# Two layers of attention with two-level fast products: outer additions queued behind VectorE's urgent reads, statistics read in attention, first factors in one transfer each

## The chip, the cores and the metric

The kernel runs on one core of one Trainium2 chip. The metric is the device time of one execution in microseconds (us): 3364.67 for the kernel before, the median of 3 runs (3364.36 to 3367.72). The profiled execution has a span of 3367.4 us.

A core has TensorE (matrix products into the accumulators of PSUM), VectorE, ScalarE and GpSimd, which work at the same time, each through its own list of instructions in the order in which the program gives them, and transfers (DMA), which are issued from a list of their own, SyncE's. In the profile they are PE (and PEld for the loading of weights), DVE, ACT, POOL and SP.

## The reference

Eight samples of 512 channels by 32 x 32 positions go through two attention layers. A layer is, cut to what matters:

```python
xn  = group_norm(x)                        # 8 groups of 64 channels, over all positions
q, k, v = wq @ xn + bq, wk @ xn + bk, wv @ xn + bv
attn = softmax(q_head . k_head * scale)    # 8 heads of 64 channels, 1024 x 1024 each
out  = attn . v_head
x    = x + wp @ out + bp
```

Everything is fp32. A sample in a layer is a *job*; the 16 jobs run in the order (sample 0, layer 0), (1, 0), (0, 1), (1, 1), (2, 0) and so on, so that the job two places after one in layer 0 is the same sample in layer 1.

## The kernel before

The four projections of a job are computed with Strassen-like products: a product of matrices of 2 x 2 blocks with 7 block products and additions of the factors before and of the results after. V and the output projection do it once. K and Q do it twice: seven outer products, each a *chain* of seven inner products. The sums of the weights (*factors*) are made once per layer and kept in HBM.

One job's stages: attention of job n; the V products of job n+1; the output projection of job n; the K and Q products of job n+1 (14 chains). One instruction list of VectorE serves all of this. `later` and `advance` are a plan in Python, without effect on the chip: they decide at which place in the program's order an operation is put.

The chains of K and Q. `step` does one inner product and the reading of an accumulator bank that belongs to it; products 7 and 3 are read by VectorE, the others by ScalarE:

```python
        def step(o):
            product(o, {1: z, 5: w, 6: z, 2: y, 7: z, 3: u, 4: z}[o], o in (1, 5))
            if o == 1:
                nc.scalar.copy(y, z)
            elif o == 5:
                put5(w)
            elif o == 6:
                nc.scalar.copy(u, z)
            elif o == 2:
                put(0, 0, y)
            elif o == 7:
                put(1, 1, z)        # VectorE
            elif o == 3:
                put(0, 1, u)        # VectorE
            else:
                put(1, 0, z)        # ScalarE
```

Each chain's result is a tile of pool `e`; the *outer additions* put these results together into k or q as soon as a chain has ended:

```python
        def end(c):
            ...
            if o == 2:
                nc.vector.tensor_add(quarter(0, 0), p(1), p(2))
            elif o == 6:
                nc.vector.tensor_add(p(6), p(6), p(1))
            elif o == 5:
                nc.vector.tensor_add(quarter(0, 1), p(6), p(5))
            elif o == 7:
                nc.vector.tensor_add(p(7), p(7), p(6))
                nc.vector.tensor_add(quarter(1, 1), p(7), p(5))
            ...
        def thunk(c, j):
            def go():
                if j == 0:
                    live[c] = begin(c)
                live[c](ORDER[j])        # ORDER = (1, 5, 6, 2, 7, 3, 4)
                if j == 6:
                    end(c)
                advance(0.43)
            return go

        at = sorted((7 * c + 2 * j, c, j) for c in range(len(chains)) for j in range(7))
```

By the last line the chains overlap: after the end of chain c (place 7c+12) come product 2 of chain c+1 (7c+13), product 1 of c+2, product 7 of c+1 (7c+15), product 5 of c+2, product 3 of c+1 (7c+17).

Results of chains and the exponentials of attention share one pool of buffers:

```python
    epool = ctx.enter_context(tc.tile_pool(name="epool", bufs=LEAD + 2))   # LEAD = 2
    ...
            e = epool.tile([P, 2, HALF], F32, tag="e", name=f"e_{n}_{i}")
            nc.scalar.activation(e, sc, AF.Exp, scale=SCALE)
```

The inner factors of K and Q are made when a layer is first met (jobs 0 and 2): the pieces are fetched from the stored outer factors, four small additions on VectorE make the rest (`prepare`), and the whole is stored:

```python
    def fetch():
        if not plan:
            return
        ...
        if which in (V, O):
            nc.sync.dma_start(wide(w), src)
        elif (which, layer, o) in deep:
            nc.sync.dma_start(w, deep[which, layer, o])
        else:
            for at, i, j in ((A11, 0, 0), (A12, 0, 1), (A22, 1, 1), (S3, 1, 0)):
                nc.sync.dma_start(w[:, at], src[:, j, i * P : (i + 1) * P])
            raw.add(key)
```

In job 0 the outer factors are made on the way, too. Raw K, raw Q and the finished k are tiles with the same tag "k" of a pool with one buffer: each needs the one before to be done with. The same holds for raw V and q (tag "q"):

```python
    store_factors(v0, 0, V)
    first_blocks(k0, 0, K, 0.1)
    deep_sums(0, 7.0, 14.0)

    def second_blocks():
        q0 = acts.tile([P, NW, 2, CH], F32, tag="k", name="raw_q0")
        load_blocks(q0, 0, Q)
        first_blocks(q0, 0, Q, 6.0)
    ...
    later(7.5, first_plan)      # fetches K's seven pieces
    later(9.0, second_blocks)
```

The statistics of the next job's normalisation (four times two readings of 128 x 512 and one small operation) are put into attention for a job in layer 0, and among the chains before it for a job in layer 1:

```python
            reads, steps = norm_steps(n + 2)
            if jobs[n + 2][1] == 1:
                for i, step in enumerate(reads):
                    later(9.0 + 6.0 * i, step)
                reads = []
        ...
                chores = dict(zip((4, 8, 12, 16), reads))    # in attention
```

Of the kernel before, what the change touches and what calls it, by code (L numbers as in the profile page):

```python
# [18 lines left out]
P = 128  # L19
# [14 lines left out]
LEAD = 2  # L34
RP = 32
NQ = P // RP
CH = C // 2
A11, A12, A22, S1, S2, S3, S4 = range(7)
NW = 7
K, V, Q, O = range(4)  # L40
FACTOR = {1: A11, 2: A12, 3: S4, 4: A22, 5: S1, 6: S2, 7: S3}
# [28 lines left out]
def fast_path(  # L70
# [10 lines left out]
    nc = tc.nc  # L81
    xpool = ctx.enter_context(tc.tile_pool(name="xpool", bufs=2))
    acts = ctx.enter_context(tc.tile_pool(name="acts", bufs=1))
    epool = ctx.enter_context(tc.tile_pool(name="epool", bufs=LEAD + 2))
    apool = ctx.enter_context(tc.tile_pool(name="apool", bufs=2))
    small = ctx.enter_context(tc.tile_pool(name="small", bufs=2))
    dram = ctx.enter_context(tc.tile_pool(name="dram", bufs=2, space=DRAM))
# [19 lines left out]
    def advance(us):  # L107
        clock[0] += us
        due = [t for t in todo if t[0] <= clock[0]]
        for t in due:  # L110
            todo.remove(t)
            t[1]()
# [18 lines left out]
    def raw_block(layer, which, i, j):  # L131

        if which == O:
            w, at = wp[layer], 0
        else:
            w, at = wqkv[layer], {Q: 0, K: C, V: 2 * C}[which]
        cols = slice(at + i * CH, at + (i + 1) * CH)
        return w[j * CH : (j + 1) * CH, cols].rearrange("(cc p) o -> p cc o", p=P)
# [1 line left out]
    factors, deep = {}, {}  # L140

    def load_blocks(w, layer, which):
        for at, i, j in ((A11, 0, 0), (A12, 0, 1), (A22, 1, 1), (S3, 1, 0)):
            nc.sync.dma_start(w[:, at], raw_block(layer, which, i, j))

    def factor(w, part):

# [16 lines left out]
    def fetch():  # L164


        if not plan:
            return
        key = plan.popleft()
        n, which, o = key  # L170
        layer = jobs[n][1]
        w = ring.tile([P, NW, P], F32, tag="w", name=f"w_{which}_{n}_{o}")
        held[key] = w
        src = factors[which, layer][:, FACTOR[o]]
        if which in (V, O):
            nc.sync.dma_start(wide(w), src)
        elif (which, layer, o) in deep:
            nc.sync.dma_start(w, deep[which, layer, o])
        else:
            for at, i, j in ((A11, 0, 0), (A12, 0, 1), (A22, 1, 1), (S3, 1, 0)):  # L180
                nc.sync.dma_start(w[:, at], src[:, j, i * P : (i + 1) * P])
            raw.add(key)

    def prepare(key):
# [257 lines left out]
    def deep_phases(n):  # L442


        layer = jobs[n][1]
        dst = {}
        chains = [(K, o) for o in OUTER] + [(Q, o) for o in OUTER]
        tiles = {}

        def begin(c):  # L450
            which, o = chains[c]
            if o == OUTER[0]:
                name = "k" if which == K else "q"
                dst[which] = acts.tile([P, NC, S], F32, tag=name, name=f"{name}_{n}")
                (kt if which == K else qt)[0] = dst[which]
            if c + 2 < len(chains):
                prepare((n,) + chains[c + 2])
            e = epool.tile([P, 2, HALF], F32, tag="e", name=f"p_{n}_{c}")
            tiles[which, o] = e
            s5 = small.tile([P, QT], F32, tag="s5", name=f"s5_{n}_{c}", bufs=3)  # L460
            half = c % 2
            z, y, u, w = (
                bank(half, b, f"{b}d_{n}_{c}")[:, :QT] for b in ("vyuz", "zyuv")[(c // 2) % 2]
            )
            r = right(xn[0], tx[0], o)
            if o in (4, 5, 6):
                sums = deep_t[0][:, :, {5: 0, 6: 1, 4: 2}[o], :]
            else:
                at = {1: 0, 7: 1, 2: 2, 3: 3}[o]
                sums = deep_x[0][:, :, at, :]  # L470
            moving = {
                1: r[:, 0, :QT], 2: r[:, 1, :QT], 3: r[:, 1, QT:],
                5: sums[:, 0, :], 6: sums[:, 1, :], 7: sums[:, 2, :], 4: sums[:, 3, :],
            }
            lhs = held[n, which, o]

            def bias(oo):
                if o in (1, 6, 7):
                    return None
                if o == 3:  # L480
                    return bias_step[:, layer, int(which == Q), oo : oo + 1]
                oc = oo if o == 2 else 2 + oo
                return env.vec(layer, BK if which == K else BQ, oc)

            def product(i, ps, start):
                nc.tensor.matmul(  # L486
                    ps, lhs[:, FACTOR[i], :], moving[i], start=start, stop=True,
                    skip_group_check=True,
                )

            def put(oo, ph, ps):
                to_ = e[:, oo, ph * QT : (ph + 1) * QT]
                b = bias(oo)
                if ph == 0:
                    if b is None:
                        nc.scalar.copy(to_, ps)
                    else:
                        nc.scalar.activation(to_, ps, AF.Identity, bias=b)
                elif b is None:
                    nc.vector.tensor_add(to_, ps, s5)  # L500
                else:
                    nc.vector.scalar_tensor_tensor(to_, ps, b, s5, ALU.add, ALU.add)  # L502

            return chain(product, lambda ps: nc.scalar.copy(s5, ps), put, z, y, u, w)

        def end(c):
            which, o = chains[c]
            used((n, which, o))
            d = dst[which]

            def quarter(oh, sh):
                return d[:, 2 * oh : 2 * oh + 2, sh * HALF : (sh + 1) * HALF]

            def p(k):
                return tiles[which, k]

            if o == 2:
                nc.vector.tensor_add(quarter(0, 0), p(1), p(2))
            elif o == 6:
                nc.vector.tensor_add(p(6), p(6), p(1))  # L520
            elif o == 5:
                nc.vector.tensor_add(quarter(0, 1), p(6), p(5))
            elif o == 7:
                nc.vector.tensor_add(p(7), p(7), p(6))  # L524
                nc.vector.tensor_add(quarter(1, 1), p(7), p(5))
            elif o == 3:
                nc.vector.tensor_add(quarter(0, 1), quarter(0, 1), p(3))
            elif o == 4:
                nc.vector.tensor_add(quarter(1, 0), p(7), p(4))

        live = {}

        def thunk(c, j):
            def go():
                if j == 0:
                    live[c] = begin(c)
                live[c](ORDER[j])
                if j == 6:
                    end(c)
                advance(0.43)  # L540

            return go

        at = sorted((7 * c + 2 * j, c, j) for c in range(len(chains)) for j in range(7))
        return [thunk(c, j) for _, c, j in at]
# [181 lines left out]
    def first_blocks(w, layer, which, delay):  # L727

        for part in range(4):
            later(delay + 1.7 * part, lambda part=part: factor(w, part))  # L730
        later(delay + 6.0, lambda: store_factors(w, layer, which))

    def make_out_bias(w, layer):

        pb = two_banks("sc", f"pb_{layer}")
        for oc in range(NC):
            i, o0 = oc // 2, (oc % 2) * P
            for cc in range(NC):
                at = {(0, 0): A11, (0, 1): A12, (1, 0): S3, (1, 1): A22}[i, cc // 2]
                nc.tensor.matmul(  # L740
                    pb[:, 0, oc : oc + 1], w[:, at, cc % 2, o0 : o0 + P],
                    env.vec(layer, BV, cc), start=(cc == 0), stop=(cc == NC - 1),
                )
        a0 = layer * NVEC + BP
        nc.vector.tensor_add(out_bias[:, layer, :], pb[:, 0, :NC], env.vec_sb[:, a0 : a0 + NC])
# [51 lines left out]
    for step in (  # L797
# [1 line left out]
        lambda: factor(v0, 3), t[3],  # L799
    ):  # L800
        step()
    store_factors(v0, 0, V)
    first_blocks(k0, 0, K, 0.1)
    deep_sums(0, 7.0, 14.0)

    def second_blocks():
        q0 = acts.tile([P, NW, 2, CH], F32, tag="k", name="raw_q0")
        load_blocks(q0, 0, Q)
        first_blocks(q0, 0, Q, 6.0)

    def first_plan():
        plan.extend((0, K, o) for o in OUTER)
# [2 lines left out]

    def second_plan():
        plan.extend((0, Q, o) for o in OUTER)
        fetch()

    later(7.5, first_plan)  # L820
    later(9.0, second_blocks)
    for thunk in first[4:-1]:
        thunk()
    advance(0.0)
    rest = first[-1:]
    for n in range(-1, len(jobs)):
# [48 lines left out]
        reads = steps = []  # L875
        if n + 2 < len(jobs):
            reads, steps = norm_steps(n + 2)
            if jobs[n + 2][1] == 1:
                for i, step in enumerate(reads):
                    later(9.0 + 6.0 * i, step)  # L880
                reads = []
        for i, thunk in enumerate(both[1:-3]):
            if n < 0 and i == 14:
                second_plan()
            thunk()
        att_n = n + 1
# [252 lines left out]
```

## Time and profile before

| | |
|---|---|
| time, median of 3 runs | 3364.67 us |
| span of the profiled execution, mean granted TensorE clock | 3367.4 us, 0.995 |
| TensorE busy | 3286.2 us, 98% of the span |
| VectorE busy | 2602.4 us, 77% |
| ScalarE busy | 1727.5 us, 51% |
| moved by DMA | 262.83 MB, 78 GB/s over the span |
| chain of work that ended last | TensorE 90%, VectorE 6%, ScalarE 2%, DMA 1% |
| scores and values of attention in that chain | 26% and 25% |
| issues of pieces of K's and Q's factors (fetch) | 112 of 64 KB |

Busy time of an engine is the union of its instructions. In a group of instructions the idle time stands before them, with what ended it; a line of the timeline has its start, its length, engine, line of the program, tiles (out<-in), shapes, a count where neighbours are merged, and in brackets the engine's idle time before it and what it waited for. DMA issues stand on SyncE's queue (SPq); what they move lands later.

### The profile page before, as it was taken

The page shows a single profiled execution, that of the slowest core. Times are in us where ns is not written, and L with a number is a line of the kernel's source. Part 1 is how long each engine was busy: PE and PEld are TensorE (multiplying, and loading weights), DVE is VectorE, ACT ScalarE, POOL GpSimd, SP SyncE. Part 2 cuts the span into 40 slices and gives each one's busy share as a digit, 9 for nine tenths or more (in the row PEclk, how much of TensorE's full clock was granted, in tenths as well). Part 3 has the DMA queues.
Part 4 walks back from the last instruction along what each step waited for, and adds up shares of the span by engine and source line. Part 5 has one row for each costly group of instructions (what it writes and reads, how often), then busy time and mean ns, then how long its engine had stood idle before and what let it go on. Part 6 is the DMA issues. An engine that isn't in the chain of part 4 may idle for free.

```text
span 3367.4 us, 56688 instructions
## 1 busy us (share of the span) xinstructions
PE 3286.2 (98%) x22420; PEld 1742.5 (52%) x22420; DVE 2602.4 (77%) x3630; ACT 1727.5 (51%) x2557; POOL 17.5 (1%) x30
## 2 busy tenths in 40 slices
PE   7999999999999999999999999999999999999999
PEld 5446364463655636456374553735546365463643
DVE  6796977959688686786968869687795977968676
ACT  2554635646365463655636456363663635546363
POOL 0000000000000000000000000000000000000000
PEclk8999999999999999999999999999999999999999
DMA  6224132140411303114050220303215031130401
GB/s 237 91 84 130 62 105 86 57 160 18 129 60 41 101 22 100 38 51 138 22 161 28 66 75 22 115 24 96 93 34 161 18 89 50 40 102 18 125 29 44
DMA packets 154450, 262.83 MB, mean 78 GB/s; under 512 B 45888, under 2 KB 68416, under 8 KB 153152
## 3 DMA queue, kind: packets, MB, share of 16 engines
q1 hardware_dynamic: 154176, 259.12, 24.8%
q8 instruction: 178, 2.92, 0.4%
q14 instruction: 96, 0.79, 0.1%
HBM read 212.10 MB, written 44.83 MB: 76 GB/s over the span
## 4 chain that ended last, share of the span: by engine, by line
PE 90%; DVE 6%; ACT 2%; DMA 1%; issue 1%; SPq 0%; POOL 0%; DVEq 0%; ACTq 0%; POOLq 0%
PE sc L593 26%; PE po L618 25%; PE vd L486 6%; PE z L384 6%; PE z L419 6%; PE zd L486 6%; PE yd L486 2%; PE ud L486 2%; ACT e L598 2%; PE v L384 2%; PE y L384 2%; PE u L384 2%; PE y L419 2%; PE u L419 2%; PE v L419 2%; DVE p L524 1%
## 5 line engine op out<-in xcount | busy, mean ns | idle before, releaser
L598 ACT ACTIVATE e<-sc 128x1024 f32<-128x1024 f32 x1024 | 1045.7, 1023 | 640.9 <-PE sc L593 515.4
L593 PE MATMUL sc<-q,k 64*64 64x512 f32 x8192 | 1071.6, 593 | 16.0 <-ACT e L598 16.0
L618 PE MATMUL po<-e,v 64*64 64x512 f32 x8192 | 1060.2, 590 | 0.0
L604 DVE TENSOR_TENSOR acc<-acc,e 128x1024 f32<-128x1024 f32 x768 | 937.2, 1220 | 83.0 <-ACT e L598 32.6
L618 PEld LDWEIGHTS po<-e,v 64*64 64x64 f32 x8192 | 313.4, 134 | 568.4 <-issue 557.4
L593 PEld LDWEIGHTS sc<-q,k 64*64 64x64 f32 x8192 | 304.3, 133 | 563.1 <-issue 517.0
L486 PE MATMUL vd<-deep,w 128*128 128x256 f32 x960 | 278.0, 387 | 47.1 <-DVE p L502 30.6
L602 DVE TENSOR_TENSOR acc<-e,e 128x1024 f32<-128x1024 f32 x128 | 156.5, 1223 | 115.6 <-ACT e L598 114.4
L486 PE MATMUL zd<-deep,w 128*128 128x256 f32 x832 | 235.5, 383 | 6.9 <-DVE p L500 3.5
L486 PEld LDWEIGHTS vd<-deep,w 128*128 128x128 f32 x960 | 178.5, 191 | 99.3 <-DVE p L502 43.5
L486 PEld LDWEIGHTS zd<-deep,w 128*128 128x128 f32 x832 | 156.2, 190 | 43.2 <-DVE p L502 8.5
L630 DVE TRANSPOSE_TENSOR_REDUCE r<-acc 128x32 f32<-128x1024 f32 x128 | 158.5, 1238 | 0.6
L335 ACT COPY yd<-vd 128x256 f32<-128x256 f32 x128 | 45.7, 357 | 185.5 <-PE vd L486 178.2
L426 DVE TENSOR_TENSOR s5o<-v,x 128x512 f32<-128x512 f32 x60 | 38.6, 684 | 100.4 <-PE v L419 100.4
L419 PE MATMUL z<-to,w 128*128 128x512 f32 x240 | 110.4, 593 | 0.0
L384 PE MATMUL z<-w,xn 128*128 128x256 f32 x480 | 110.1, 383 | 0.0
L384 PE MATMUL z<-w,t 128*128 128x256 f32 x480 | 108.5, 379 | 0.0
L419 PE MATMUL z<-q,w 128*128 128x512 f32 x240 | 107.9, 593 | 0.0
L660 DVE TENSOR_TENSOR q<-q,rb 128x512 f32<-128x512 f32 x128 | 86.6, 677 | 27.5 <-DMA rb<-rd 27.5
L384 PEld LDWEIGHTS z<-w,xn 128*128 128x128 f32 x480 | 90.1, 190 | 23.7 <-issue 12.2
L384 PEld LDWEIGHTS z<-w,t 128*128 128x128 f32 x480 | 91.4, 190 | 12.2
L339 ACT COPY u<-z 128x512 f32<-128x512 f32 x62 | 35.3, 570 | 121.5 <-PE z L419 84.8
(176 smaller groups left out, 3434.7 us busy)
## 6 DMA issues: line engine op xcount, KB each, us to landing
w<-deep SPq DMA_DIRECT2D x196, 448.0 KB, 3.4
w<-keep SPq DMA_DIRECT2D x210, 256.0 KB, 2.7
rb<-rd SPq DMA_DIRECT2D x256, 128.0 KB, 2.9
x<-x_dram SPq DMA_DIRECT2D x32, 512.0 KB, 5.8
out_dram<-x SPq DMA_DIRECT2D x64, 256.0 KB, 3.6
deep<-w SPq DMA_DIRECT2D x28, 448.0 KB, 2.7
keep<-raw SPq DMA_DIRECT2D x5, 1792.0 KB, 5.9
lr<-r SPq DMA_DIRECT2D x512, 4.0 KB, 1.7
```

What stands on the lines that cost most here:

```text
L335: nc.scalar.copy(y, z)
L384: nc.tensor.matmul(ps[:, ti * CH : (ti + 1) * CH], r[:, cc, t0 : t0 + P], w[:, cc, :], start=(start and ti == 0 and cc == 0), stop=(cc == ...
L419: nc.tensor.matmul(ps, w[:, cc, i * P : (i + 1) * P], r[:, cc, :], start=(start and cc == 0), stop=(cc == 1), skip_group_check=True,)
L426: nc.vector.tensor_add(s5[:, oh, :], ps, at(oh, 1))
L486: nc.tensor.matmul(ps, lhs[:, FACTOR[i], :], moving[i], start=start, stop=True, skip_group_check=True,)
L593: nc.tensor.matmul(sc[h * HD : (h + 1) * HD, j, :], k[r, hp, k0 : k0 + HD], q[r, hp, sh * HALF : (sh + 1) * HALF], start=True, stop=True,)
L598: nc.scalar.activation(e, sc, AF.Exp, scale=SCALE)
L602: nc.vector.tensor_add(acc[g], es[i - 1], e)
L604: nc.vector.tensor_add(acc[g], acc[g], e)
L618: nc.tensor.matmul(po[g][j * HD : (j + 1) * HD, h, :], v[r, kc, d0 : d0 + HD], e[r, j, :], start=(kc == 0), stop=(kc == NT - 1),)
L630: nc.vector.tensor_reduce(r, a.rearrange("p j (b e) -> p (j b) e", e=RP), AX.X, ALU.add, apply_transpose=True,)
L660: nc.vector.tensor_mul(q[:, hp, cols], q[:, hp, cols], rb)
```

## The change

It leaves the computation as it is and touches the order and the transfers:

1. Outer additions are not given to VectorE at a chain's end. They go into a queue, and one is taken from it after each read of product 7 or 3 of the chains that follow, so that a read for which TensorE waits does not stand behind an addition for which nobody does. The rest is done at the end of the last chain. As results live longer, pool `e` gets a fifth buffer.
2. The statistics are read in attention for all jobs.
3. The blocks of a stored factor lie in the order in which a piece is used, so that a piece comes with one transfer, not four. In job 0 the order is another: K's outer factors are made at once, V's are stored much later, Q's blocks are loaded before K's pieces are fetched, and Q's pieces are fetched later and as many as the ring holds.

```diff
-A11, A12, A22, S1, S2, S3, S4 = range(7)
+A11, S3, A12, A22, S1, S2, S4 = range(7)
...
-    epool = ctx.enter_context(tc.tile_pool(name="epool", bufs=LEAD + 2))
+    epool = ctx.enter_context(tc.tile_pool(name="epool", bufs=LEAD + 3))
...
     def load_blocks(w, layer, which):
-        for at, i, j in ((A11, 0, 0), (A12, 0, 1), (A22, 1, 1), (S3, 1, 0)):
-            nc.sync.dma_start(w[:, at], raw_block(layer, which, i, j))
+        for i in range(2):
+            for j in range(2):
+                nc.sync.dma_start(w[:, 2 * j + i], raw_block(layer, which, i, j))
...
-        if not plan:
+        if not plan or len(held) == RING:
             return
...
         else:
-            for at, i, j in ((A11, 0, 0), (A12, 0, 1), (A22, 1, 1), (S3, 1, 0)):
-                nc.sync.dma_start(w[:, at], src[:, j, i * P : (i + 1) * P])
+            nc.sync.dma_start(wide(w), src)
             raw.add(key)
...
+            def add(to_, a, b):
+                outer.append(lambda: nc.vector.tensor_add(to_, a, b))
+
             if o == 2:
-                nc.vector.tensor_add(quarter(0, 0), p(1), p(2))
+                add(quarter(0, 0), p(1), p(2))
   ... (the other additions likewise)
         live = {}
+        outer = deque()
         def thunk(c, j):
             def go():
                 if j == 0:
                     live[c] = begin(c)
                 live[c](ORDER[j])
+                if ORDER[j] in (7, 3) and outer:
+                    outer.popleft()()
                 if j == 6:
                     end(c)
+                    if c + 1 == len(chains):
+                        while outer:
+                            outer.popleft()()
                 advance(0.43)
...
-        later(delay + 6.0, lambda: store_factors(w, layer, which))
+        later(delay + 5.3, lambda: store_factors(w, layer, which))
...
-    store_factors(v0, 0, V)
-    first_blocks(k0, 0, K, 0.1)
-    deep_sums(0, 7.0, 14.0)
+    for part in range(4):
+        factor(k0, part)
+    store_factors(k0, 0, K)
+    deep_sums(0, 0.5, 7.5)
...
-        first_blocks(q0, 0, Q, 6.0)
+        first_blocks(q0, 0, Q, 8.0)
...
     def second_plan():
         plan.extend((0, Q, o) for o in OUTER)
-        fetch()
-
-    later(7.5, first_plan)
+        while len(held) < RING and plan:
+            fetch()
+
+    later(12.0, first_plan)
     later(9.0, second_blocks)
+    later(35.0, lambda: store_factors(v0, 0, V))
...
-            if jobs[n + 2][1] == 1:
-                for i, step in enumerate(reads):
-                    later(9.0 + 6.0 * i, step)
-                reads = []
         for i, thunk in enumerate(both[1:-3]):
-            if n < 0 and i == 14:
+            if n < 0 and i == 28:
                 second_plan()
             thunk()
```

More of the change, by code (lines that the diff above doesn't have):

```diff
@@ L515, in p @@
                 return tiles[which, k]
+            def add(to_, a, b):
+                outer.append(lambda: nc.vector.tensor_add(to_, a, b))
             if o == 2:
-                nc.vector.tensor_add(quarter(0, 0), p(1), p(2))
+                add(quarter(0, 0), p(1), p(2))
             elif o == 6:
-                nc.vector.tensor_add(p(6), p(6), p(1))
+                add(p(6), p(6), p(1))
             elif o == 5:
-                nc.vector.tensor_add(quarter(0, 1), p(6), p(5))
+                add(quarter(0, 1), p(6), p(5))
             elif o == 7:
-                nc.vector.tensor_add(p(7), p(7), p(6))
-                nc.vector.tensor_add(quarter(1, 1), p(7), p(5))
+                add(p(7), p(7), p(6))
+                add(quarter(1, 1), p(7), p(5))
             elif o == 3:
-                nc.vector.tensor_add(quarter(0, 1), quarter(0, 1), p(3))
+                add(quarter(0, 1), quarter(0, 1), p(3))
             elif o == 4:
-                nc.vector.tensor_add(quarter(1, 0), p(7), p(4))
+                add(quarter(1, 0), p(7), p(4))
         live = {}
+        outer = deque()
         def thunk(c, j):
@@ L738, in make_out_bias @@
             for cc in range(NC):
-                at = {(0, 0): A11, (0, 1): A12, (1, 0): S3, (1, 1): A22}[i, cc // 2]
+                at = 2 * (cc // 2) + i
                 nc.tensor.matmul(
```

## The prediction

> **What bounds the kernel now.** I read the page first: the busy shares and the slices say which engine sets the pace.
>
> ```profile
> PE 3286.2 (98%) x22420; PEld 1742.5 (52%) x22420; DVE 2602.4 (77%) x3630; ACT 1727.5 (51%) x2557; POOL 17.5 (1%) x30
> PE   7999999999999999999999999999999999999999
> ```
>
> TensorE hardly stops, so only its pauses can be won; work saved or moved on another engine counts through them alone. The list of waits names them, with a count that tells how often each comes (16 is once per job):
>
> ```profile
> ACT e L598 <- DVE q L529: 41.5, 16, 2.6
> PEld vd L486 <- DVE p L502: 43.5, 32, 2.6
> DVE raw_q L149 <- DMA raw_q<-wqkv_dram: 10.2, 1, 10.2
> ```
>
> Then I cut the trace into stages by TensorE's lines and asked for the busy time of four product stages (the 14 chains that make k and q): jobs 3, 5, 2 and 0.
>
> ```profile
> 706.57:753.08 46.51, 44.94 (x212) 36.82 (x210) 27.97 (x41) 28.07 (x70) 0.00 (x0) 1.00 0.50 169
> 1117.38:1165.09 47.71, 45.69 (x211) 36.56 (x210) 32.73 (x53) 28.06 (x70) 0.00 (x0) 1.00 0.36 106
> 485.83:540.55 54.72, 47.07 (x212) 36.10 (x210) 43.56 (x104) 27.97 (x70) 0.00 (x0) 1.00 0.57 186
> 42.91:113.06 70.15, 48.98 (x212) 37.54 (x210) 43.35 (x100) 28.46 (x71) 0.00 (x0) 0.90 0.62 201
> ```
>
> After the stretch stands its length, then busy time and count of TensorE, its weight loads, VectorE and ScalarE; near the end the granted clock, DMA share and GB/s. The same matmuls take 46.5, 47.7, 54.7 and 70.2 us. Undisturbed, one product (L486) starts every 0.43 us; 14 x 7 of them with the two score steps of 0.86 us make about 43.9 us. Seven jobs look like the first row, seven like the second (there VectorE also reads the next job's statistics), job 2 and job 0 stand alone. The other stages have little to give: values 24.3 us, output products 24.5 us, attention 110.2 us with one pause at its start.
>
> The pause of the common stage, in the timeline of job 3 (start, length, engine, line):
>
> ```profile
> 745.35 1.23 DVE L524 TENSOR_TENSOR p<-p,p 128x1024 f32<-128x1024 f32 x1 [0.84 <-ACT p L496]
> 746.61 1.23 DVE L525 TENSOR_TENSOR q<-p,p 128x1024 f32<-128x1024 f32 x1
> 747.76 0.48 DVE L502 SCALAR_TENSOR_TENSOR p<-vd,bias_step,s 128x256 f32<-128x256 f32 x1
> 748.29 0.70 PE L486 MATMUL vd<-deep,w 128*128 128x256 f32 x2 [0.79 <-DVE p L502]
> ...
> 754.93 1.23 DVE L529 TENSOR_TENSOR q<-p,p 128x1024 f32<-128x1024 f32 x1
> 756.25 1.94 ACT L598 ACTIVATE e<-sc 128x1024 f32<-128x1024 f32 x2 [2.59 <-DVE q L529]
> 757.33 1.09 PE L593 MATMUL sc<-q,k 64*64 64x512 f32 x8 [0.59 <-ACT e L598]
> ```
>
> VectorE waits 0.84 us for ScalarE's last read of the chain, makes the two outer additions of product 7 in a row, and only then reads the next chain's bank (L502), for which TensorE stands still. Below: the third exponential of the attention gets no buffer until the last outer addition (L529) frees one.
>
> For job 0 the timeline shows a chain of transfers (SPq lines are DMA issues):
>
> ```profile
> 36.20 13.56 SPq L181 DMA_DIRECT2D w<-keep  x28
> 49.80 1.97 SPq L144 DMA_DIRECT2D raw_q<-wqkv_dram  x4
> ...
> 56.95 0.69 DVE L149 TENSOR_TENSOR raw_q<-raw_q 128x512 f32<-128x512 f32 x1 [10.18 <-DMA raw_q<-wqkv_dram]
> ...
> 60.56 1.22 PE L486 MATMUL vd<-deep,w 128*128 128x256 f32 x2 [14.04 <-DVE p L500]
> ```
>
> 28 issues of 0.48 us hold back the loading of Q's blocks; VectorE stands 10.2 us in front of them, TensorE 14.0 us behind VectorE.
>
> [...] a waiting addition blocks the bank read behind it. The trace agrees (0.84 us above, then TensorE's 0.79). [...] the pieces here are 64 KB and cost 0.48 us of issue each, against a median 0.32 for a whole one of 256 KB in L176. [...] here, after 14.0 us of standing, products start 0.85 us apart until 64.5 us and 0.43 after.
>
> **Part 1, outer additions.** Each goes behind the read of product 7 or 3 of the next chain, three or five products (1.3 or 2.2 us) after its chain's end. By then ScalarE's read is done, so the 0.9 us wait goes, and the urgent read comes before 1.23 us of addition. The read behind the addition (product 3's bank) is next wanted a chain or more later. Pauses that go:
> - Jobs 3, 4, 7, 8, 11, 12, 15: two per stage (K and Q, product 7), each 0.95 us against regular starts plus 0.10 for the restart: 2.1 us. 7 x 2.1 = 14.8.
> - Jobs 1, 5, 6, 9, 10, 13, 14: 1.51 + 1.05 + 3 x 0.25 = 3.3 us, 1.2 of it from statistics. 7 x 3.3 = 23.2.
> - The fifth e buffer lets the third exponential start before L529. TensorE's loss there is 0.75 us from start to start, once per attention: 16 x 0.75 = 12.0. The fourth exponential may then wait some 0.3 us for L529, but a score bank is free and TensorE should not notice.
>
> **Part 2, statistics in attention.** Four times two readings and a small one, 1.45 us each, move from the product stage into steps 4 to 16 of the attention. Attention takes 110.15 us in job 3, where these reads are in it already (VectorE 101.99 us busy, 138 instructions), and 110.16 in job 5, where they are not (96.54, 126), so I charge nothing. The gain is in the 3.3 above.
>
> **Part 3, first factors.** Q's blocks are loaded as soon as K's stored factors have landed and free the buffer (now 36.2; some 2.5 us earlier without V's store ahead), before K's pieces, which become 7 transfers. Issues then take about 2.0 + 7 x 0.35 = 4.5 us, not 15.5. Q's blocks land near 40 us, before VectorE wants them near 44. In job 0, the starts that are late add to 25.9 us: 14.2 for the stand, 2.2 for half clock, 9.5 for ten smaller pauses of 0.7 to 2.0 behind outer additions and four preparing operations per chain. The first 16.4 go. Something comes back: the first addition into k needs the buffer of Q's raw factors, which is free only when their store has landed. I expect its issue near 50 us and 5.7 us for it (as now), so landing near 56; the addition comes up near 51.5. TensorE can run some eleven products (4.7 us) before it needs VectorE, and VectorE needs about 3 us more to catch up: a pause of 3 to 4 us. Of the 9.5, about 2 remain: preparing (0.94) + addition (1.14) + two reads (0.75) = 2.8 us per chain against TensorE's 3.02, which fits, except where product 7 has two additions. Left 5.5, won 20.4.
> Job 2 has 10.3 us of such pauses, no load to wait for, and loses its statistics too: left 1.0, won 9.3. K's and Q's pieces there become 14 transfers as well.
>
> **Sum:** 14.8 + 23.2 + 12.0 + 20.4 + 9.3 = 79.7. I take off 1.7 for new short waits: 3364.67 - 78 = 3286.7 us.
>
> **Rivals.**
> - The additions only move the pause: they hold product 3's read, and preparing meets them. For it: VectorE is 93% busy by the 2.8 above wherever it prepares. Against: 27.97 of 46.51 us in the common stage, and the bank held is not the next one. It would leave half of job 0's and job 2's small pauses, some 6 us more: 3293.
> - The store of Q's factors takes the place of the load. For it: in the trace VectorE waits for this store too (2.0 us), and the new order brings the addition nearer to it; stores of 448 KB per chain and fetches of 256 KB ask for some 240 GB/s beside it, where the highest slice of the page shows 237. If it lands at 61 rather than 56, another 5 us and half clock for a while: 3294.
> - Attention pays for the statistics, or its first pause stays because buffers come free in another order. For it: VectorE is 93% busy there. Against: job 3, in which it is so already. It would cost up to 12 us: 3299.
> - First transfers hidden: Q's load first makes K's first piece late for the start of job 0 (now 40.75 us), 1 to 3 us.
>
> **Range and chances.** The steady pauses (50 us) repeat to 0.01 us in every job and have one visible cause; job 0 (20) is the loose part, +-5, job 2 +-3, attention -6. That gives 3278 to 3302 for 8 in 10. The 2% line is at 3297.4, below which 67 of the 80 us must come true; two rivals together would miss it. Faster by over 2%: 0.80; within: 0.18; slower: 0.02.
>
> **What would show it.** Right: product stages near 44.5 us in jobs 1 and 3 alike; no TensorE wait on L529; no stand of 14 us and no half clock near 60 us; 84 fewer issues; attention still 110 less 0.75. Wrong: outer additions that wait for Q's store longer than 6 us, attention longer than 110 us in jobs 1 or 5, TensorE waiting for the reads of product 3, or job 2's stage above 48 us.

## The result, and the profile after

The changed kernel takes 3290.43 us, the median of 4 runs (3284.87 to 3292.88), against 3364.9 (3364.36 to 3367.72, 4 runs): a ratio of 0.9775, 95% interval 0.9758 to 0.9792. Measured again for the last experiment, it was 3291.96 against 3366.88, 0.9777 (0.9763 to 0.979). The prediction was 3286.7, range 3278 to 3302: 78 us were foretold and some 75 came.

The page of the changed kernel: TensorE's and the other engines' busy time, TensorE's 40 slices, the chain that ended last by engine.

```profile
PE 3265.8 (99%) x22420; PEld 1748.7 (53%) x22420; DVE 2588.4 (79%) x3630; ACT 1729.2 (53%) x2557; POOL 17.5 (1%) x30
PE   8999999999999999999999999999999999999999
PE 97%; ACT 1%; DMA 1%; DVE 1%; issue 0%; SPq 0%; POOL 0%; DVEq 0%
```

No instruction has gone from any of the computing engines, and the 112 issues of 64 KB for the pieces of K's and Q's factors have become 28 of 256 KB. The chain that ended last ran over VectorE for 6% of the span and does for 1% now. The product stages of jobs 3, 5, 2 and 0, with the columns as in the prediction (length, busy time of TensorE, weight loads, VectorE, ScalarE; clock, DMA share and GB/s at the end):

```profile
674.49:718.88 44.39, 44.39 (x211) 36.93 (x209) 26.83 (x41) 28.06 (x70) 0.00 (x0) 1.00 0.52 175
1079.45:1123.85 44.40, 44.40 (x211) 36.92 (x209) 26.84 (x41) 28.06 (x70) 0.00 (x0) 1.00 0.38 115
464.11:509.28 45.17, 44.92 (x211) 36.71 (x209) 37.84 (x92) 27.97 (x70) 0.00 (x0) 1.00 0.66 225
45.91:96.19 50.28, 46.62 (x212) 37.94 (x210) 39.01 (x93) 28.46 (x71) 0.00 (x0) 0.97 0.68 246
```

In the first two TensorE's busy time is the length of the stage: there is no pause left. Job 2 keeps 0.8 us, job 0 keeps 5.9. How the steady pause went, in the timeline of job 3:

```profile
714.64 0.48 DVE L502 SCALAR_TENSOR_TENSOR p<-ud,bias_step,s 128x256 f32<-128x256 f32 x1
715.03 1.22 DVE L518 TENSOR_TENSOR q<-p,p 128x1024 f32<-128x1024 f32 x1
...
716.91 0.48 DVE L502 SCALAR_TENSOR_TENSOR p<-vd,vec_sb,s 128x256 f32<-128x256 f32 x1 [0.67 <-PE vd L486]
717.32 1.21 DVE L518 TENSOR_TENSOR q<-q,p 128x1024 f32<-128x1024 f32 x1
...
720.74 1.23 DVE L518 TENSOR_TENSOR q<-p,p 128x1024 f32<-128x1024 f32 x1
...
722.06 1.03 ACT L607 ACTIVATE e<-sc 128x1024 f32<-128x1024 f32 x1 [1.00 <-DVE q L518]
722.37 1.04 PE L602 MATMUL sc<-q,k 64*64 64x512 f32 x8
```

Now VectorE waits for TensorE (0.67 us ahead of a read) and each addition (all have line 518 now) follows a read at once. At the start of attention it is the fourth exponential that waits for the last addition, 1.00 us, and TensorE goes on without a pause behind it.

Job 0, from the timelines of the DMA issues, VectorE and TensorE:

```profile
24.56 0.33 SPq L160 DMA_DIRECT2D keep<-raw_v  x1
28.22 0.33 SPq L160 DMA_DIRECT2D keep<-raw_k  x1
36.71 1.92 SPq L145 DMA_DIRECT2D raw_q<-wqkv_dram  x4
38.68 3.73 SPq L181 DMA_DIRECT2D w<-keep  x7
...
43.67 0.67 PE L486 MATMUL vd<-xn,w 128*128 128x256 f32 x2 [1.53 <-DMA w<-keep]
...
53.26 0.32 SPq L160 DMA_DIRECT2D keep<-raw_q  x1
...
59.06 1.23 DVE L518 TENSOR_TENSOR k<-p,p 128x1024 f32<-128x1024 f32 x1 [4.33 <-DMA keep<-raw_q]
...
62.00 0.70 PE L486 MATMUL zd<-deep,w 128*128 128x256 f32 x2 [3.41 <-DVE p L502]
```

The stand of 14 us is gone. Two smaller ones have come: 1.53 us for K's first piece, before the stage begins, and 3.41 us behind the store of Q's factors. After the second one TensorE runs at half clock for 3.41 us, from 63.20 to 66.61 (the 0.50 is the granted clock):

```profile
64.00:66.00 2.00, 2.00 (x6) 1.63 (x5) 1.72 (x4) 0.61 (x2) 0.00 (x0) 0.50 0.90 328
```

### The profile page after: what moved, and what is told of

It reads as the page before. It is cut to its first block, busy times and chain, and to the rows that moved or that the text cites. A ratio compares the mean times of both kernels' runs of the same rounds, so it can differ in the third digit from the quotient of the medians.

```text
span 3289.6 us, 56485 instructions
## 1 busy us (share of the span) xinstructions
PE 3265.8 (99%) x22420; PEld 1748.7 (53%) x22420; DVE 2588.4 (79%) x3630; ACT 1729.2 (53%) x2557; POOL 17.5 (1%) x30
## 4 chain that ended last, share of the span: by engine, by line
PE 97%; ACT 1%; DMA 1%; DVE 1%; issue 0%; SPq 0%; POOL 0%; DVEq 0%
PE sc L602 27%; PE po L627 26%; PE vd L486 8%; PE zd L486 7%; PE z L384 6%; PE z L419 6%; PE ud L486 3%; PE yd L486 3%; PE u L384 2%; PE y L384 2%; PE v L384 2%; PE u L419 2%; PE y L419 2%; PE v L419 2%; ACT e L607 1%; PE pp L571 1%
## 5 line engine op out<-in xcount | busy, mean ns | idle before, releaser
L613 DVE TENSOR_TENSOR acc<-acc,e 128x1024 f32<-128x1024 f32 x768 | 936.5, 1219 | 60.6 <-ACT e L607 11.0
L486 PE MATMUL vd<-deep,w 128*128 128x256 f32 x960 | 269.7, 382 | 0.0
```

The source lines that it names most:

```text
L486: nc.tensor.matmul(ps, lhs[:, FACTOR[i], :], moving[i], start=start, stop=True, skip_group_check=True,)
L613: nc.vector.tensor_add(acc[g], acc[g], e)
```

## The experiments

All stages are cut as in the prediction, from a stage's first product to the next one's, each in one profile. "Time" is the median of the runs, or the only run. Jobs 5 and 3 stand for the seven stages with and without statistics before. Seven rows are single runs (fifth buffer, statistics, not joined, no queue, V's store late, Q's factors early, statistics back). The changed kernel's own runs lie 8 us apart, so times as close as that are not ranked here; the stages are compared instead. The kernel before, run beside the three groups of experiments, had medians of 3366.57, 3365.91 and 3366.88. Attention of job 0 depends on the half clock in its profile (last section: 6.83 us of it in the changed kernel's 116.47), so it does not rank the parts.

| kernel | time | job 0 starts | job 0 | job 5 | job 3 | job 2 | attention job 3 | attention job 0 |
|---|---|---|---|---|---|---|---|---|
| before | 3364.67 | 42.91 | 70.15 | 47.71 | 46.51 | 54.72 | 110.16 | 117.32 |
| changed | 3290.43 | 45.91 | 50.28 | 44.40 | 44.40 | 45.18 | 109.34 | 116.47 |
| part 1 alone | 3300.66 | 43.30 | 60.84 | 44.40 | 44.40 | 48.47 | 109.34 | 114.81 |
| fifth buffer alone | 3352.44 | 43.47 | 69.22 | 47.71 | 46.51 | 54.73 | 109.34 | 113.17 |
| statistics alone | 3355.11 | 42.65 | 69.21 | 46.51 | 46.51 | 53.05 | 110.16 | 115.68 |
| joined pieces alone | 3359.45 | 42.81 | 61.36 | 47.72 | 46.50 | 55.62 | 110.87 | 113.99 |
| changed, pieces not joined | 3296.3 | 46.04 | 55.90 | 44.40 | 44.40 | 45.16 | 109.34 | 114.86 |
| changed, no queue | 3338.7 | 47.24 | 60.53 | 46.50 | 46.50 | 53.03 | 109.34 | 116.49 |
| changed, V's store late | 3287.26 | 44.97 | 50.28 | 44.40 | 44.40 | 45.17 | 109.45 | 116.45 |
| changed, raw Q in x buffer | 3287.09 | 45.07 | 49.03 | 44.40 | 44.40 | 45.17 | 109.54 | 116.46 |
| ... and Q's factors early | 3286.32 | 46.45 | 45.49 | 44.40 | 44.40 | 45.17 | 109.55 | 114.86 |
| changed, statistics back | 3294.46 | 45.39 | 50.30 | 44.40 | 44.40 | 48.44 | 109.60 | 116.46 |
| early factors, bias spread | 3283.73 | 44.63 | 44.91 | 44.40 | 44.40 | 45.18 | 109.61 | 115.37 |
| changed, again | 3291.96 | 46.48 | 50.30 | 44.40 | 44.40 | 45.18 | 109.34 | 116.46 |

### The parts one by one

**Part 1 alone**: the kernel before with the queue and the fifth buffer.

```diff
-    epool = ... bufs=LEAD + 2
+    epool = ... bufs=LEAD + 3
...
+            def add(to_, a, b):
+                outer.append(lambda: nc.vector.tensor_add(to_, a, b))
  ... (all outer additions through add)
+                if ORDER[j] in (7, 3) and outer:
+                    outer.popleft()()
  ... (at the end of the last chain the rest)
```

> The kernel before with part 1 alone (queue of outer additions, five e buffers). Theory (the reads stand behind the additions, and nothing else does): common product stages 46.50 to 44.40 us; stages with statistics 47.71 to 44.4-45.0, since the statistics alone fit between the reads; job 2's stage 54.7 to about 46.5; attention 110.16 to 109.34; job 0 keeps its stand of 14 us, its stage falls from 70.2 to about 61. Sum 7 x 2.1 + 7 x 3.0 + 8 + 16 x 0.82 + 9 = 66: near 3299 us. Rival (the additions move the pause, and statistics meet them): the seven stages with statistics stay near 47.7, near 3320 us.

It took 3300.66 us against 3366.57, ratio 0.9807 (0.979 to 0.9823). The seven stages with statistics fall to 44.40 although the statistics are still in them. Window of job 5's stage and a piece of VectorE's timeline in it:

```profile
1085.53:1129.93 44.40, 44.40 (x212) 36.86 (x210) 32.04 (x53) 28.07 (x70) 0.00 (x0) 1.00 0.39 115
```
```profile
1100.32 1.22 DVE L518 TENSOR_TENSOR k<-p,p 128x1024 f32<-128x1024 f32 x1
1101.45 0.42 DVE L500 TENSOR_TENSOR p<-ud,s 128x256 f32<-128x256 f32 x1
1101.79 1.28 DVE L223 BATCH_NORM_STATS2 stats<-x 128x6 f32<-128x512 f32 x2
1103.10 0.21 DVE L224 BATCH_NORM_AGGREGATE mv<-stats 128x2 f32<-128x12 f32 x1
1103.22 0.43 DVE L502 SCALAR_TENSOR_TENSOR p<-vd,bias_step,s 128x256 f32<-128x256 f32 x1
1103.57 1.22 DVE L518 TENSOR_TENSOR p<-p,p 128x1024 f32<-128x1024 f32 x1
```

Addition, statistics, read and addition stand edge to edge and TensorE does not stop (busy 44.40 of 44.40 us). The rival, that the additions only move the pause, is out for these stages. Job 2's stage is 48.47, not 46.5; the statistics account for it, as the run with them put back shows below.

**The fifth buffer alone** (`bufs=LEAD + 3` in the kernel before).

> The kernel before with a fifth e buffer and nothing else. Theory (the pause at the start of attention is the third exponential without a buffer): attention 110.16 to 109.34 us in every job, product stages as before (46.50 and 47.71), about 3352 us. Rival (the pause comes from the place of the last outer addition, or the new buffer goes to another tile): attention stays at 110.16, 3365 us.

Attention falls from 110.16 to 109.34, the product stages stay: the pause at its start was the buffer, and all of it.

**Statistics alone** (the three lines that put them among the chains taken out of the kernel before).

> The kernel before with the statistics read in attention for all jobs and nothing else. Theory: seven product stages 47.71 to 46.50 us, job 2's 54.7 to 52-53, attention unchanged at 110.16 (up to 0.3 us more in job 1, where factors are made as well), about 3354 us. Rival (attention pays): attention above 110.5 us in jobs 1, 5, 6, 9, 10, 13, 14, and no gain in sum.

46.51 in all fourteen stages, 53.05 in job 2, attention 110.16 in job 3; 110.39 in job 1, where factors are made as well. One run, 3355.11: as expected.

**Joined pieces alone**: the blocks' places and one transfer per piece in the kernel before, its order in job 0 kept.

```diff
-A11, A12, A22, S1, S2, S3, S4 = range(7)
+A11, S3, A12, A22, S1, S2, S4 = range(7)
...
-            for at, i, j in (...): nc.sync.dma_start(w[:, at], src[:, j, i * P : (i + 1) * P])
+            nc.sync.dma_start(wide(w), src)
```

> The kernel before with a piece's four transfers joined to one and the order of job 0 as it was. Theory (28 issues hold back the loading of Q's blocks): 7 issues instead, Q's blocks land near 46 us instead of 57, the stand of 14 us and the half clock go, a pause of 3 to 4 us for the store of Q's factors comes; job 0's product stage 70.2 to about 55.5, about 3350 us. Rival (the order is what counts: Q's blocks still stand behind K's pieces and K's store): the stage stays above 65 us, over 3360 us.

The ratio is 0.9979 (0.9972 to 0.9987), about 7 us; job 0's stage takes 61.36, between what theory and rival had said. Its issues and VectorE:

```profile
36.08 3.17 SPq L180 DMA_DIRECT2D w<-keep  x7
39.29 2.30 SPq L144 DMA_DIRECT2D raw_q<-wqkv_dram  x4
...
47.11 0.69 DVE L149 TENSOR_TENSOR raw_q<-raw_q 128x512 f32<-128x512 f32 x1 [0.67 <-DMA raw_q<-wqkv_dram]
```

Q's blocks come at 47.1, an us later than reckoned, and VectorE hardly waits for them. But the sums and preparing operations that the old order puts there as well keep VectorE busy, and TensorE stands for 4.3 us until 50.7, then for 1.9 us until 60.6 behind Q's store. The rest I put down to the additions at the chains' ends; this was not measured. Nor was it traced why attention of job 3 takes 110.87 us in this one profile.

**Changed kernel, pieces not joined** (the four transfers per piece put back).

> The changed kernel with four transfers per piece again (its order of job 0 kept). Theory (once Q's blocks are loaded ahead of them, the many issues cost little): a piece every 1.9 us, the third one some 1 to 3 us later for VectorE; job 0's product stage 50.3 to 51-53 us, job 2's unchanged at 45.2, about 2 us more than the changed kernel. Rival (joining carries part 3): job 0's stage above 56 us or job 2's above 47.

Job 0's stage takes 5.6 us more, where I had expected 1 to 3, and stays just under the rival's 56; job 2's takes no more. The few lines that say why (issues, VectorE, TensorE):

```profile
39.11 14.14 SPq L182 DMA_DIRECT2D w<-keep  x28
53.34 3.90 SPq L195 DMA_DIRECT2D deep<-w  x5
57.33 1.08 SPq L160 DMA_DIRECT2D keep<-raw_q  x1
...
65.02 1.23 DVE L519 TENSOR_TENSOR k<-p,p 128x1024 f32<-128x1024 f32 x1 [8.85 <-DMA keep<-raw_q]
...
67.96 1.22 PE L487 MATMUL zd<-deep,w 128*128 128x256 f32 x2 [7.93 <-DVE p L503]
```

The 28 issues no longer hold back Q's loading, which is ahead of them; they hold back the stores behind them. Q's store is issued 4.1 us later than at 53.26 and takes 1.9 us longer to land.

What order and joining are worth apart is shown in part only. With the queue, job 0's stage ends at 104.14 us in the old order (part 1 alone), at 101.94 in the new order and at 96.19 with joined pieces as well. Without the queue it ends at 104.17 with joined pieces alone and at 107.77 with the new order added: there the order brings nothing. Joined pieces with the queue in the old order were not run, so it stays open whether the new order is needed. Each of these ends is from one profile, and in the changed kernel's half clock alone accounts for 1.7 us (3.41 us at 0.50).

**Changed kernel without the queue** (additions at the chain's end again, the rest kept).

> The changed kernel with the outer additions at each chain's end again (five e buffers, statistics in attention and part 3 kept). Theory: all fourteen steady product stages 44.40 to 46.50 us, job 2's 45.2 to about 52, job 0's 50.3 to about 58, attention stays at 109.34 because that gain is the buffer's; about 44 us more than the changed kernel, near 3335. Rival (the attention gain needs the queue's order): attention 110.16, near 3347.

All three kinds of stage come back near what was expected (46.50, 53.03, 60.53; for job 0 some 58 had been expected), and attention stays at 109.34. The one run took 3338.7 us, some 47 more than the changed kernel, three more than expected.

**Changed kernel, statistics back among the chains.**

> The changed kernel with the statistics of layer 1 among the chains again (part 2 undone). Theory (once the reads go ahead of the additions, statistics are in nobody's way except where VectorE also prepares): the seven stages stay at 44.40 us, job 2's goes from 45.2 to about 48.5, attention of job 1 from 109.57 to 109.34; about 3 us more than the changed kernel. Rival (they meet the reads even so): the seven stages go to 45.5 or more, 8 us or more in sum.

The seven stages stay at 44.40, job 2's goes to 48.44: part 2 is worth 3.3 us there and 0.2 us against it in attention of job 1. The rest of what the statistics cost before had gone with part 1.

### What is left in job 0

**V's store really late.** In the trace of the changed kernel V's store is still issued at 24.56, ahead of K's, though the program plans it 35 us after its place: the kernel fixes the order for TensorE, VectorE and ScalarE alone (`manual_schedule`). That SyncE's list was arranged by what is ready was my guess; the trace shows only where the store was issued. An operation on one element makes V's factors ready late, and with it the store is issued at 69.45:

```diff
-    later(35.0, lambda: store_factors(v0, 0, V))
+    def store_v():
+        corner = v0[0:1, S4, 1, CH - 1 : CH]
+        nc.vector.tensor_copy(corner, corner)
+        store_factors(v0, 0, V)
+    later(35.0, store_v)
```

> The changed kernel with V's store really late: one VectorE operation on one element of V's factors (copied onto itself) is put ahead of the store at its planned place, so that the store can't be issued at 24.6 us ahead of K's. Theory (V's store ahead of K's delays K's landing, then Q's blocks and K's pieces): K's store lands 2 to 2.5 us earlier, near 34; TensorE's wait of 1.5 us for the first piece goes, the product stage of job 0 starts near 44 instead of 45.9; the pause of 3.4 us for Q's store stays. Rival (the piece comes late because it stands behind Q's blocks): the wait stays above 1 us.

```profile
28.17 0.33 SPq L160 DMA_DIRECT2D keep<-raw_k  x1
36.00 1.92 SPq L145 DMA_DIRECT2D raw_q<-wqkv_dram  x4
...
42.62 0.29 DVE L150 TENSOR_TENSOR w<-w 128x128 f32<-128x128 f32 x1 [1.30 <-DMA w<-keep]
...
58.08 1.23 DVE L518 TENSOR_TENSOR k<-p,p 128x1024 f32<-128x1024 f32 x1 [4.29 <-DMA keep<-raw_q]
```

Q's loading starts at 36.00 instead of 36.71, not 2.5 us earlier, and TensorE still waits 1.3 us for the first piece. My theory fell: K's store takes 7.8 us from issue to landing without V's ahead, 8.5 with it, so V's store costs it only 0.7 us. The rival stands, that the first piece is late behind Q's blocks; the next run, in which Q's blocks are out of the way, supports it.

**Raw Q in the second x buffer**, so that neither Q's loading waits for K's buffer nor k for Q's store; sample 1 is loaded later into it.

```diff
...
-        q0 = acts.tile([P, NW, 2, CH], F32, tag="k", name="raw_q0")
+        q0 = xpool.tile([P, NC, S], F32, tag="x", name="raw_q0")   # 7 of its 8 parts used
...
+        later(38.0, next_x)       # touches one element of q0, then load_x(1)
...
```

> The changed kernel with raw Q in the second x buffer, which sample 1 needs only from its statistics on (its loading is put after the store of Q's factors, behind a VectorE operation on one element); k's buffer is then free at once. Theory (the pause of 3.4 us and the half clock behind it are the wait of the first addition into k for Q's store; the first piece stands behind Q's blocks): both go, with the 1.5 us at the start; job 0's product stage starts near 43.7 and takes 44.5 to 45.5 us instead of 50.3, about 3283 us. Rival (VectorE's backlog or Q's pieces take its place): the stage stays above 47 us.

3287.09 us against 3365.91, 0.9763 (0.9747 to 0.9779). TensorE does not wait for the first piece any more, and no addition waits for the store; but the stage is 49.03, as the rival had it:

```profile
52.42 0.32 SPq L160 DMA_DIRECT2D keep<-raw_q  x1
58.19 2.62 SPq L181 DMA_DIRECT2D w<-keep  x5
...
62.04 0.29 DVE L150 TENSOR_TENSOR w<-w 128x128 f32<-128x128 f32 x1 [3.53 <-DMA w<-keep]
...
63.45 0.70 PE L487 MATMUL vd<-deep,w 128*128 128x256 f32 x2 [2.67 <-DVE p L501]
```

Two waits hung on one store. With the first taken away, the second shows 3 us later: Q's pieces are fetched only when the store has landed (58.2), and VectorE stands for the first of them until 62.0.

**Q's factors early.** The same, with Q's blocks loaded right behind K's and the factors made during the V products, so that their store does not come late.

```diff
-    later(9.0, second_blocks)
+    second_blocks()
...
-        first_blocks(q0, 0, Q, 8.0)
+        first_blocks(q0, 0, Q, 0.1)
...
+        later(52.0, next_x)
```

> The changed kernel with raw Q in the second x buffer (as in the run before), loaded right behind raw K, and its factors made right behind K's, in the V products, so that their store is issued some 20 us earlier (near 32 us). Theory (what is left in job 0's product stage is the way store, landing, fetch of Q's pieces, preparing, whose first step is late): Q's store has landed near 40 us, VectorE waits for no transfer in the stage, the stage takes 44.5 to 45.5 us (50.3 in the changed kernel, 49.0 with the buffer alone), starts near 44, and the half clock behind the pause goes; about 3283 us. Rival (the transfers of the stage, some 250 GB/s, are themselves too slow): some piece is waited for again and the stage stays above 47 us.

The stage takes 45.49 us, and no transfer is waited for within it. Q's store is issued at 34.7, two to three us later than expected, and lies ahead of K's pieces instead of Q's blocks: TensorE waits 2.16 us for the first one and begins the stage at 46.45, not 44. The stage ends at 91.94 instead of 96.19. The transfers within the stage are fast enough for these 45.49 us; the rival is out.

**The spread, and a kernel that beats both.** The changed kernel's runs lie 8 us apart, its first profile shows half clock, apart from the start (15.41 to 22.24 us) and the end (from 3288.80), in three places: at 63.20 us behind the 3.41 us pause, and at 121.23 and 534.24 within the 32 one-column products of the output bias in attention of jobs 0 and 2, which begin at 118.66 and 531.76; there it lasts 6.83 us. The last kernel makes Q's factors early and puts the 32 products into four places, three steps apart:

```diff
-                chores[at] = lambda i=i, layer=layer: make_out_bias(box[0][:, i], layer)
+                for oc in range(NC):
+                    chores[at + 3 * oc] = lambda i=i, layer=layer, oc=oc: make_out_bias(
+                        box[0][:, i], layer, [oc])
  ... (and the edits of the run before)
```

> As with Q's factors made early, and the 32 one-column products of the output bias in attention of jobs 0 and 2 put into four places three steps apart, not one. Theory (one-column products in a row let the granted clock fall to half for up to 3.3 us behind them, by chance more or less, which is also the spread of the runs): attention of jobs 0 and 2 takes 113 to 114 us in every run, not 113.2 to 117.3, minus about 4 us, and the spread shrinks; median near 3279 us, some 10 less than the changed kernel. Rival (the clock falls for another reason, or the three further turns of a score bank cost as much): attention of jobs 0 and 2 stays near 116.

The changed kernel beside it on the same chip:

> The changed kernel as it is, on the same chip, to compare with. Theory: 3290 us, with runs from 3284 to 3293 and the mean granted clock lower where the time is higher; its product stages 44.40 us again. Rival (its spread comes from transfers): the granted clock is the same in fast and slow runs.

3283.73 us (3283.36 to 3285.3, 5 runs) against 3291.96 (3289.77 to 3292.58, 5 runs): 8 us less, no run of one within the range of the other. In all nine runs of the changed kernel the time follows the mean clock: 3291.33 to 3292.88 us with 0.996 (six runs), 3289.53 and 3289.77 with 0.997, 3284.87 with 0.998. A window in attention of job 0 of the changed kernel, then job 0's product stage and a window in its attention of the last kernel (the third figure from the end is the clock):

```profile
124.00:128.00 4.00, 4.00 (x21) 1.40 (x25) 0.94 (x2) 1.02 (x1) 0.00 (x0) 0.50 0.06 16
```
```profile
44.63:89.54 44.91, 44.66 (x211) 36.84 (x209) 36.84 (x90) 28.49 (x71) 0.00 (x0) 1.00 0.80 280
120.00:128.00 8.00, 7.71 (x71) 3.23 (x74) 7.64 (x12) 3.11 (x4) 0.00 (x0) 1.00 0.02 2
```

The clock holds: all five runs have a mean of 0.999, those of the changed kernel beside it 0.996 to 0.997. Early factors alone did not do it: attention of job 2 still takes 116.49 us there, and the mean clock of the run is 0.997. But attention of jobs 0 and 2 falls only from 116.46 to 115.37, not to 113 to 114. With the 32 products in one place it took 113.17 in three profiles (job 0 with the fifth buffer alone, job 2 in two others), which is near the changed kernel's 116.47 less the 3.4 us that 6.83 us at 0.50 cost it; so I estimate that the spreading itself costs 2.2 us. Of these, 1.0 are waits at the new places (0.71 for an addition of the bias, 0.29 for an exponential), as the rival had it; where the rest goes was not traced. So most of the 8 us is job 0, whose product stage ends at 89.54 instead of 96.78.

## Why the prediction was right, and where it was off

From the two profiles (spans 3367.4 and 3289.6, 77.8 apart), with the terms of the sum:

| term | foretold | measured |
|---|---|---|
| seven common stages | 7 x 2.1 = 14.8 | 7 x 2.11 = 14.8 |
| seven with statistics | 7 x 3.3 = 23.2 | 7 x 3.31 = 23.2 |
| attention | 16 x 0.75 = 12.0 | 15 x 0.82 + 0.59 = 12.9 |
| job 0 | 20.4 | 113.06 - 96.19 = 16.9 |
| job 2 | 9.3 | 54.72 - 45.18 = 9.5 |
| new short waits | -1.7 | none outside job 0 |

These are 77.3; the other half us is in the last projection. The medians are some 75 apart, not 78, for the profiled run of the kernel before (3369.14 us) was slower than all its other runs. That 77.8 comes so near 78 is partly luck: job 0 brought 3.5 us less than reckoned, and the 1.7 us set aside, the 0.9 us more of attention and the half us of the last projection made up for it.

- **Steady pauses.** Right to a tenth, and shown by taking the queue in and out. The reason "a waiting addition blocks the bank read behind it" holds: with the additions at the chains' ends again the common stage went from 44.40 back to 46.50 us. But I counted the 1.2 us of statistics per stage as part 2's gain; part 1 alone takes it all (44.40 with the statistics still in the stage). The two gains overlap: parts 1 and 2 each alone bring 66 and 11 us, and part 2 on top of the others brings 3.
- **Attention.** Right: the buffer alone brings 0.82, which I had as 0.75. The fourth exponential waits 1.00 us instead of my 0.3, and as foretold TensorE does not notice. "So I charge nothing" for the statistics was right except for 0.23 us in job 1.
- **Job 2.** 0.8 us left where I said 1.0.
- **Job 0**, 3.5 us less than reckoned. The step that failed is "some 2.5 us earlier without V's store ahead". V's store stayed ahead, and when it was really put off, K's store landed only 0.7 us earlier. So Q's loading starts at 36.7 instead of some 33.7, the issues of the pieces take 0.53 us each and not 0.35, K's first piece is waited for 1.5 us, and everything behind it in job 0 comes later, Q's store too (53.26, not near 50). The stage itself gains 19.9 us, near the 20.4, but it starts 3.0 us later: the 1.5, 0.3 by which the V products begin later, and about 1 us more that they lose to half clock at the start (granted clock 0.78 over 16 to 30 us, 0.85 before). Whether the change has a part in this last is open: over the same 14 us two other kernels with the changed start have 0.83 (V's store late) and 0.74 (raw Q in the x buffer), and no wait in the traces tells why. The "pause of 3 to 4 us" for Q's store came with 3.41, but I left out that half clock follows it, 3.41 us at 0.50, which costs 1.7 us. Against that, of the 9.5 us of small pauses about 0.5 were left and not 2.
- **Rivals.** The store did take the place of the load, in the small size of the sum and not that of the rival. Attention paid 0.2 us, in job 1. The additions did not move the pause. The late first piece, which the sum had left out, came with 1.5 us.

## What to carry to other kernels

When one engine's list serves urgent reads and leisurely work, put the leisurely work behind a read that waits anyway: here the stages with statistics went from 47.71 to 44.40 us with the statistics still in the list, and these, for which I had charged 1.2 us, cost nothing there once the additions were out of the way. A store that is both the release of a buffer and the source of the next load carries two waits: here, taking one away showed the other 3 us later, and it was the earlier store that removed both. Before crediting a planned delay, look in the trace at the place where the transfer was really issued: V's store, planned late, was issued at 24.56 us.

## What the runs showed that I had not expected

- The same pause was followed by half clock in one kernel and not in another. In the profiles of the kernel before and of the changed one the stretches of half clock from 20 us on begin at 50.81, 139.56, 566.23 and 3365.16 us, and at 63.20, 121.23, 534.24 and 3288.80: within each profile whole multiples of 3.413 us apart (121.23 and 534.24, for instance, 121 steps). They last 3.41, 6.83 or 13.65 us, one, two or four steps, but for the last ones, which reach the end of the program. The same pause of 2.15 us comes in job 2 of two kernels. In the kernel before, the end of a step at 508.20 cuts it into 0.69 and 1.46 us, and the clock stays at 1.00; with joined pieces alone it ends at 497.36, just ahead of a step, and that step, from 497.86, runs at 0.50 (job 2's stage takes 55.62 us there, 54.72 before):

```profile
509.66 0.70 PE L486 MATMUL vd<-deep,w 128*128 128x256 f32 x2 [2.15 <-DVE p L502]
508.20:511.61 3.41, 1.95 (x9) 1.75 (x10) 2.47 (x8) 1.20 (x3) 0.00 (x0) 1.00 0.48 172
...
497.36 0.77 PE L485 MATMUL vd<-deep,w 128*128 128x256 f32 x2 [2.15 <-DVE p L501]
497.86:501.28 3.42, 3.42 (x9) 2.72 (x9) 2.52 (x6) 1.30 (x3) 0.00 (x0) 0.50 0.60 197
```

  In the kernel before, the step at 47.40 us, all of it a pause, was followed by half clock, and those at 67.88 and 508.20, with 1.64 and 1.46 us of pauses, were not. In the changed kernel the step at 59.79, with 2.21 us of pauses, was, and the one at 56.37, with 1.20 us, was not. Nothing in the traces tells why.
- TensorE was busy in other steps that half clock followed. In the changed kernel the 32 one-column products begin at 118.66 us and the granted clock falls to 0.50 at 121.23, with TensorE busy in all of the 4.23 us before; in the kernel before they begin at 136.35 and it falls at 139.56. In both it stays there for 6.83 us, two steps, which cost 3.4 us. With the fifth buffer and these products in one place, attention of job 0 took 113.17, 114.8 to 114.9 or 116.4 to 116.5 us, the same products each time; the values lie some 1.65 us apart, which I take for no, one and two steps of half clock at 1.7 us each, an estimate from the two steps in the changed kernel's 116.47. Without the buffer it took up to 117.32.
- In the packets of the trace 15 of the 16 last writes of K's store came by 34.2 us in the changed kernel, the sixteenth at 35.7, directly behind a packet of 16 KB of the instruction queue (34.7 to 35.7). Whether that packet held the write back the records do not say.
